# One transfer for the opening's weights, and x of stage 3's first 16 rows put together during stage 2

## The chip, the cores and the metric

The kernel runs on one core of a Trainium2 chip. The metric is the device time of one execution in microseconds (us). In what follows PE is TensorE, DVE VectorE, ACT ScalarE, POOL GpSimd and SP SyncE; SP, ACT and POOL also issue transfers (DMAs), each in the order of its own queue.

## What is computed

The input x has 384 x 384 positions of 128 channels in float32. Two layers follow one another:

```python
# layer 0
z = layernorm(x, norm_g, norm_b)
left  = (z @ Wl + bl) * sigmoid(z @ Wlg + blg)
right = (z @ Wr + br) * sigmoid(z @ Wrg + brg)
core = einsum('bikh,bjkh->bijh', left, right)
zo = layernorm(core, onorm_g, onorm_b) @ Wout + bout
x = x + sigmoid(x @ Wg + bg) * zo
# layer 1
left  = x @ W_left + b_left + x @ W_eq + b_eq
right_sum = sum(x @ W_right + b_right, axis=2)
out = (left * right_sum * sigmoid(x @ W_gate + b_gate)) @ W_out + b_out
y = layernorm(out + x, ln_scale, ln_bias)
```

## The kernel before, in words

The work is done in three stages, and nearly every instruction is pinned behind the one before it on its engine by `seq(...)`, so each engine and each DMA queue works in the order of the program.

**Stage 1** (0 to 1131 us) normalizes x and makes left and right for all 128 heads. It takes x in 288 steps of four rows by 128 positions. For each step DVE takes the statistics, POOL the reciprocal root (`powers`) and subtracts the mean (`shift`, or `first_step` for the first one), PE transposes four blocks and multiplies them by the weights `wz` (L331), ACT takes the sigmoid and DVE the product. The transposed, mean-free x goes to `xt_d` in HBM (`store_zt`), the subtracted values to `nd_d` (`store_nd`); x transposed is the sum of the two. Before the first step `fold` puts the layer norm's scale and shift into the weights. It needs the four weight matrices (`wst`), their biases (`brow`), and scale and shift as columns. Scale and shift come as two rows (`gb`), and PE turns them into columns (`pgb`, L165); DVE makes `g0`, their difference `d` and the matrix `m1` (L166 to L168); four small matmuls (L171, L172) follow, and `weights` (L179) writes `wz`. PE is kept going meanwhile with matmuls on a constant (`busy`, L156).

**Stage 2** (1131 to 1875 us) computes the core, one head h after the other: 18 matmul instructions (nine products, each recorded as two) at L501, 5.8 us a head. `load_h` (L93, L94, on SP) fetches left and right of a head three heads ahead into `lrh`; `fill` on POOL copies the right half into `rr` (L482, L483, and L476, L477 for a part that stayed on the chip); ACT copies the result to `ct` (L510) and squares it; DVE adds it to `csum` and `csq`; SP stores `ct` to `core_d` (L517). The last head is handled apart: its first 128 rows are copied, summed and stored first (L519 to L524), and the reciprocal root for them (`variance`, `root`, `inverse`, `newton`) is taken at once; POOL stores it (L533) and then sums the other rows of the last head (L534 to L536). The tiles "ve" and "r" of the pool `rp` have three buffers each.

**Stage 3** (1875 us to the end) goes through the 384 rows, row t in step t, with a software pipeline: `front` makes the gate of layer 0 for rows up to nine ahead, `scale_core(t)` multiplies the core by its reciprocal root, `layer0(t - 2)` finishes layer 0, `gated_left(t - 3)` and later `layer1` and `norm1` do layer 1. Rows are loaded in groups of RG = 4: `load_x` (SP) and `load_core` (SP). From row 16 (TR) on, x arrives transposed: `load_x` broadcasts `nd_d` into a tile (L576), and `add_x` has POOL issue an accumulating transfer of `xt_d` onto it (L584). The first 16 rows are loaded as they are (L570), PE transposes them in `front` (L640, three transposes a row), and ACT or DVE copies them out of PSUM (L642, L644). The core of rows 0 to 3 is loaded in two parts, since the last 16 heads are written last; for these rows PE spreads the root over the partitions (`pb`, L662) and DVE multiplies (L663), for later rows POOL does (L665). All loads at the start of stage 3 stand in one order on SP:

```python
for i0 in range(0, 3 * RG, RG):
    load_x(i0)
load_core(0)
load_x(3 * RG)
load_core(RG)
```

Of the kernel before, what the change touches and what calls it, by code (L numbers as in the profile page):

```python
# [14 lines left out]
P = 128  # L15
# [4 lines left out]
def triangle_then_gated_row_kernel(ctx: ExitStack, tc: tile.TileContext, a: dict, out: bass.AP):  # L20
# [10 lines left out]


    nc = tc.nc
    x = a["x"].rearrange("b i j c -> (b i) j c")
    y = out.rearrange("b i j c -> (b i) j c")
    N, _, C = x.shape
    H = a["L0_conv_Wl"].shape[1]
    assert C == P and H == P and N % P == 0
# [6 lines left out]
    A = 9  # L45
    L = 4
    TR = 16
# [6 lines left out]
    xt_d = dpool.tile([C, N, NB, P], F32, name="xt_d")  # L54
    nd_d = dpool.tile([N, N], F32, name="nd_d")

    def seq(ins):

        return tc.keep_in_program_order(ins)
# [4 lines left out]
    def load(dst, src, queue=nc.sync):  # L64
        seq(queue.dma_start(out=dst, in_=src))
# [15 lines left out]
    with ExitStack() as ctx2:  # L81
# [17 lines left out]
        with tc.tile_pool(name="p1w", bufs=6, side="right") as wp, \  # L99
# [25 lines left out]

            stage = lrp.tile([P, H, G, 2], F32, tag="lr", name="stage").rearrange("p h i s -> p (h i s)")
            wst, brow, gb = stage[:, 0:4 * H], stage[0:1, 4 * H:8 * H], stage[0:2, 8 * H:9 * H]
            m1, d = stage[:, 9 * H:10 * H], stage[:, 10 * H:10 * H + 1]
            sides = ("l", "r", "lg", "rg")
            for n, v in enumerate(("g", "b")):  # L130
                load(gb[n:n + 1], a["L0_conv_norm_" + v].rearrange("(o h) -> o h", o=1))
            for n, w in enumerate(sides):
                load(wst[:, n * H:(n + 1) * H], a["L0_conv_W" + w], nc.scalar)
            load_chunk(0, slice(4, XR))
# [7 lines left out]
            make_identity(nc, ident)  # L142
            for n, b in enumerate(sides):
                load(brow[:, n * H:(n + 1) * H], a["L0_conv_b" + b].rearrange("(o h) -> o h", o=1), nc.gpsimd)

# [3 lines left out]
            p0, p1 = (pps.tile([P, 2, 4 * H], F32, tag="pr", name=n)[:, 0] for n in ("p0", "p1"))  # L149
            pgb = tps.tile([P, 4, P], F32, tag="pt", name="pgb")[:, 0, 0:2]  # L150
            g0 = const([P, 1], "g0")

# [7 lines left out]
            def fold():  # L160

                busy(2)
                seq(nc.tensor.matmul(pgb, lhsT=gb, rhs=ident[0:2, 0:2], start=True, stop=True))  # L165
                seq(nc.vector.tensor_copy(g0, pgb[:, 0:1]))  # L166
                seq(nc.vector.tensor_sub(d, pgb[:, 1:2], g0))
                seq(nc.vector.tensor_scalar(m1, avg, d, None, ALU.mult))  # L168

                for p, gs in zip((p0, p1), halves):  # L170
                    seq(nc.tensor.matmul(p[:, gs], lhsT=m1, rhs=wst[:, gs], start=True, stop=False))  # L171
                    seq(nc.tensor.matmul(p[:, gs], lhsT=avg[0:1, :], rhs=brow[:, gs], start=False, stop=True))  # L172
# [278 lines left out]
        with tc.tile_pool(name="p2r", bufs=2, side="right", reuse_waits="tile") as rrp, \  # L451
# [14 lines left out]
            def fill(h):  # L466

                if h < H:
# [15 lines left out]
                    if h == 0:  # L484
                        stay()

            fill(0)
            for h in range(H):
                fill(h + 1)
                t, rr = loaded2.pop(h), right.pop(h)  # L490
                pc = ps.tile([P, NB, 512], F32, tag="pc", name="pc")
# [17 lines left out]
                if h < H - 1:  # L509
                    seq(nc.scalar.copy(ct, pc[:, :, :N]))  # L510
                    seq(nc.scalar.activation(sq, ct, AF.Square))
                    seq(nc.vector.tensor_add(csum, csum, ct))  # L512
                    seq(nc.vector.tensor_add(csq, csq, sq))
                    load_h(h + 3)

                    queue = nc.sync if h < H - 3 else nc.scalar
                    seq(queue.dma_start(out=to, in_=ct))  # L517
                else:
                    seq(nc.scalar.copy(ct[:, 0], banks[0]))  # L519
                    seq(nc.scalar.activation(sq[:, 0], ct[:, 0], AF.Square))  # L520
                    seq(nc.scalar.dma_start(out=to[:16, 0], in_=ct[:16, 0]))
                    seq(nc.scalar.dma_start(out=to[16:, 0], in_=ct[16:, 0]))
                    seq(nc.vector.tensor_add(csum[:, 0], csum[:, 0], ct[:, 0]))
                    seq(nc.vector.tensor_add(csq[:, 0], csq[:, 0], sq[:, 0]))  # L524
                    seq(nc.scalar.copy(ct[:, 1:], pc[:, 1:, :N]))
                    variance(0, slice(0, N))
                    root(0)
                    inverse(0, slice(0, N))
                    newton(0, slice(0, N))
                    seq(nc.scalar.dma_start(out=to[:, 1:], in_=ct[:, 1:]))  # L530


                    seq(nc.gpsimd.dma_start(out=rstd_d[0:P, :], in_=roots[0][1]))  # L533
                    seq(nc.gpsimd.tensor_tensor(sq[:, 1:], ct[:, 1:], ct[:, 1:], ALU.mult))  # L534
                    seq(nc.gpsimd.tensor_tensor(csum[:, 1:], csum[:, 1:], ct[:, 1:], ALU.add))
                    seq(nc.gpsimd.tensor_tensor(csq[:, 1:], csq[:, 1:], sq[:, 1:], ALU.add))  # L536
# [5 lines left out]
    with ExitStack() as ctx3:  # L542
# [3 lines left out]

        xp, lp, fp, inp = pool("p3x", 6), pool("p3l", 20), pool("p3f", A), pool("p3in", 3)
        wp, sp, op, up = pool("p3w", 4), pool("p3s", 4), pool("p3out", 3), pool("p3u", 18)
        ps2, ps = pool("p3ps2", 4, space=PSUM), pool("p3ps", 4, space=PSUM)
# [6 lines left out]

        def work_x(name):

            return lp.tile([P, N], F32, tag="x", name=name)

# [5 lines left out]
        def load_x(i0):  # L566

            if i0 < TR:
                xt = xin[i0] = xp.tile([P, RG, N], F32, tag="xt", name="xn")
                seq(nc.sync.dma_start(  # L570
                    out=xt.rearrange("p i (b c) -> p i b c", b=NB),
                    in_=x[i0:i0 + RG].rearrange("i (b p) c -> p i b c", p=P),
                ))
            elif i0 < N:
                xt = xts[i0] = xp.tile([P, RG, N], F32, tag="xt", name="xt")
                seq(nc.sync.dma_start(  # L576
                    out=xt.rearrange("p i j -> p (i j)"),
                    in_=nd_d[i0:i0 + RG].rearrange("i j -> (i j)").partition_broadcast(P),
                ))
# [8 lines left out]

        def load_core(i0):
            if i0 < N:  # L590
                ct = inp.tile([P, RG, N], F32, tag="ct", name="ct")

                for hs in (slice(0, H),) if i0 > 0 else (slice(0, H - 16), slice(H - 16, H)):
                    seq(nc.sync.dma_start(out=ct[hs], in_=core_d[i0:i0 + RG, hs].rearrange("i h j -> h i j")))
                rt = None
                if i0 > 0:
# [27 lines left out]
        def front(f):  # L624

            r = rows.get(f - L)
            if r:
                pg = bank("pg")
                seq(nc.tensor.matmul(pg[:, :N], lhsT=wg0, rhs=r["xT"], start=True, stop=True))  # L629
                gT = r["gT"] = work("gT", fp)  # L630
                seq(nc.scalar.activation(gT, pg[:, :N], AF.Sigmoid, bias=bg0))  # L631
            if f < N:
                i0, n = f // RG * RG, f % RG
                if f >= TR:
                    xT = xts[i0][:, n]
                else:
                    xT = work_x("xT")
                    pxt = ps2.tile([P, 512], F32, tag="py", name="pxt") if f < A else bank("pxt")
                    for s in cols:
                        seq(nc.tensor.transpose(pxt[:, s], xin[i0][:, n, s], ident))  # L640
                    if 4 <= f < A:
                        seq(nc.vector.tensor_copy(xT, pxt[:, :N]))  # L642
                    else:
                        seq(nc.scalar.copy(xT, pxt[:, :N]))  # L644
                rows[f] = {"xT": xT}

# [20 lines left out]
        def layer0(i):  # L667
# [7 lines left out]
            seq(nc.vector.scalar_tensor_tensor(pr[:, :N], pr[:, :N], bz, r["gT"], ALU.add, ALU.mult))  # L675
            x1T = r["x1T"] = work_x("x1T")
            seq(nc.vector.scalar_tensor_tensor(
# [108 lines left out]

        for i0 in range(0, 3 * RG, RG):
            load_x(i0)
        load_core(0)
        load_x(3 * RG)  # L790
        load_core(RG)

# [4 lines left out]
        for t in range(N + 3):  # L797

            while f < min(N + L, t + max(L, A - t // 3)):
                front(f)  # L800
                f += 1
            if t % RG == 0:
                load_core(t + 2 * RG)
            if t >= 2 and fetched <= f + 16:
                load_x(fetched)
                fetched += RG
# [63 lines left out]
    "x",  # L870
    "L0_conv_norm_g", "L0_conv_norm_b", "L0_conv_Wl", "L0_conv_bl", "L0_conv_Wlg", "L0_conv_blg",
    "L0_conv_Wr", "L0_conv_br", "L0_conv_Wrg", "L0_conv_brg", "L0_conv_onorm_g", "L0_conv_onorm_b",
    "L0_conv_Wout", "L0_conv_bout", "L0_conv_Wg", "L0_conv_bg",
# [22 lines left out]
```

## Time and profile before

| what | us |
|---|---|
| median of 3 runs (3287.99 to 3289.75) | 3288.08 |
| profiled execution, its own time | 3288.67 |
| span of the profiled execution (first to last instruction) | 3286.9 |
| PE busy in it | 3266.7 |
| first matmul of stage 1's products (L331) | 11.85 |
| first matmul of stage 2 (L501) | about 1131 |
| last matmul of stage 2 ends | about 1874.75 |
| first matmul of layer 0's output (L674) | 1886.24 |
| first gate matmul of layer 1 (L691) | 1888.51 |

The span is the time from the first to the last instruction; 1.8 us lie around it. Lines such as L331 are line numbers of the kernel before. A row of the profile names the engine, the line, what is written and what is read, how often, and how long; in brackets stands how long the engine was idle before it and which engine's instruction, or which transfer, ended that wait. Matmul records overlap, since they are pipelined: at full speed one product of 128 x 384 takes PE 0.645 us.

### The profile page before, as it was taken

Reading aid. Unit: us, or ns where it says so; the run is one execution under the profiler, and the core shown is the slowest. Engines: PE = TensorE matmul, PEld = TensorE weight load, DVE = VectorE, ACT = ScalarE, POOL = GpSimd, SP = SyncE. Lnnn points to the kernel's source line nnn. Section 1 sums busy time; section 2 is a strip of 40 time slices with the busy share of each in tenths; the row PEclk is TensorE's granted clock in tenths of the full one; section 3 lists DMA queues with packets and bytes.
Section 4 is the critical chain, followed back from the end, with each engine's and each line's share of the span. In section 5 each row is a group of like instructions: output and inputs, shape, how many; then the busy total and the mean of one; then the engine's idle time right before and its main releaser. Section 6 shows DMA issues by size and latency. Waiting matters only on the chain.

```text
span 3286.9 us, 48330 instructions
## 1 busy us (share of the span) xinstructions
PE 3266.7 (99%) x12460; PEld 1989.3 (61%) x12460; DVE 2489.0 (76%) x8022; ACT 1933.7 (59%) x4056; POOL 2280.3 (69%) x3301
## 2 busy tenths in 40 slices
PE   9999999999999999999999999999999999999998
PEld 4544444444444566666666666667777777777776
DVE  7777777777777655555555688888888888888888
ACT  4555555555555533333333467677777777777776
POOL 6555555555555555556666578888888888888997
PEclk9999999999999999999999999999999999999999
DMA  6998998999999499999999999999999999999994
GB/s 164 274 278 259 276 282 259 276 280 265 271 279 271 147 280 282 285 284 282 282 282 283 285 294 266 279 276 272 273 280 277 269 278 276 272 272 274 268 253 128
DMA packets 922055, 873.71 MB, mean 266 GB/s; under 512 B 24834, under 2 KB 836868, under 8 KB 921780
## 3 DMA queue, kind: packets, MB, share of 16 engines
q1 hardware_dynamic: 906532, 796.03, 78.5%
q0 software_dynamic: 13440, 72.56, 12.8%
q8 instruction: 102, 1.67, 0.2%
q10 hardware_dynamic: 1808, 2.03, 0.2%
q14 instruction: 173, 1.42, 0.1%
HBM read 508.63 MB, written 361.89 MB: 265 GB/s over the span
## 4 chain that ended last, share of the span: by engine, by line
PE 92%; POOL 5%; ACT 1%; issue 1%; DVE 1%; DMA 0%; POOLq 0%; ACTq 0%; DVEq 0%
PE pr L331 30%; PE pc L501 22%; PE py L703 7%; PE pg L629 6%; PE pl L692 6%; PE pr L674 6%; PE pg L691 6%; PE pt L279 4%; PE py L704 3%; POOL rs L723 1%; POOL yt L773 1%; POOL cs L665 1%; ACT py L738 1%; POOL nm L726 0%; POOL rs L722 0%
## 5 line engine op out<-in xcount | busy, mean ns | idle before, releaser
L331 PE MATMUL pr<-wz,zt 128*128 128x512 f32 x2304 | 1039.9, 593 | 0.0
L340 ACT ACTIVATE sg<-pr,rs 128x256 f32<-128x256 f32 x1152 | 482.9, 470 | 497.7 <-PE pr L331 363.8
L501 PE MATMUL pc<-rr,lrh 128*128 128x384 f32 x2304 | 743.3, 486 | 0.3 <-DVE lr L342 0.3
L342 DVE SCALAR_TENSOR_TENSOR lr<-pr,rs,sg 128x256 f32<-128x256 f32 x1152 | 504.6, 480 | 267.4 <-ACT sg L340 219.0
L331 PEld LDWEIGHTS pr<-wz,zt 128*128 128x128 f32 x2304 | 414.6, 191 | 410.7 <-issue 345.2
L501 PEld LDWEIGHTS pc<-rr,lrh 128*128 128x128 f32 x2304 | 452.4, 196 | 291.4 <-issue 1.1
L738 ACT ACTIVATE py<-py,nm,rs 128x128 f32<-128x128 f32 x1149 | 493.0, 430 | 197.8 <-POOL rs L727 116.8
L703 PEld LDWEIGHTS py<-wo,u 128*128 128x128 f32 x2304 | 376.8, 191 | 97.4
L512 DVE TENSOR_TENSOR csum<-csum,ct 128x1152 f32<-128x1152 f32 x127 | 179.1, 1410 | 337.9 <-ACT ct L510 337.9
L665 POOL TENSOR_TENSOR cs<-ct,rt 128x384 f32<-128x384 f32 x380 | 426.0, 1125 | 10.7 <-DMA rt<-rstd_d 5.4
L773 POOL TENSOR_TENSOR yt<-yt,lnb 128x384 f32<-128x384 f32 x380 | 423.8, 1117 | 3.1 <-DVE yt L767 3.1
L510 ACT COPY ct<-pc 128x1152 f32<-128x1152 f32 x127 | 142.1, 1119 | 445.3 <-PE pc L501 441.6
L703 PE MATMUL py<-wo,u 128*128 128x128 f32 x2304 | 402.1, 275 | 0.0
L260 POOL TENSOR_SCALAR sd<-mv 128x8 f32<-128x8 f32 (+1 forms) x145 | 28.5, 197 | 427.4 <-DVE mv L247 427.3
L270 POOL TENSOR_TENSOR z<-xt,nd 128x512 f32<-128x512 f32 x287 | 298.7, 1041 | 36.1 <-POOL z L270 30.9
L718 DVE BATCH_NORM_STATS2 st<-py 128x6 f32<-128x128 f32 x1152 | 265.6, 286 | 68.5 <-PE py L704 66.5
L704 PE MATMUL py<-ident,x1T 128*128 128x128 f32 x1152 | 314.1, 273 | 0.0
L674 PE MATMUL pr<-cs,wc 128*128 128x384 f32 x768 | 313.9, 491 | 0.0
L692 PE MATMUL pl<-x1T,mat_L_conv_W_left 128*128 128x384 f32 x768 | 311.0, 487 | 0.9 <-ACT gT L631 0.8
L691 PE MATMUL pg<-x1T,mat_L_conv_W_gate 128*128 128x384 f32 x768 | 310.8, 487 | 1.0 <-ACT g L694 0.9
L629 PE MATMUL pg<-xt,mat_L_conv_Wg 128*128 128x384 f32 x736 | 298.9, 488 | 1.3 <-ACT gT L631 1.3
L482 POOL COPY rr<-lrh 128x768 f32<-128x768 f32 x128 | 182.7, 1427 | 160.7 <-DMA lrh<-lr_d 160.2
(134 smaller groups left out, 4898.1 us busy)
## 6 DMA issues: line engine op xcount, KB each, us to landing
lr_d<-lr SPq DMA_DIRECT2D x128, 1024.0 KB, 7.2
lrh<-lr_d SPq DMA_DIRECT2D x128, 768.0 KB, 7.8
xt_d<-zt SPq DMA_DIRECT2D x288, 256.0 KB, 5.4
xt<-in_x_dram SPq DMA_DIRECT2D x143, 512.0 KB, 6.5
ct<-core_d SPq DMA_DIRECT2D x95, 768.0 KB, 6.2
rt<-rstd_d SPq DMA_DIRECT2D x95, 768.0 KB, 7.7
out_dram<-yt SPq DMA_DIRECT2D x94, 768.0 KB, 8.8
core_d<-ct SPq DMA_DIRECT2D x125, 576.0 KB, 8.8
```

The costliest lines, as they stand in the source:

```text
L331: seq(nc.tensor.matmul(pr[:, r, :], lhsT=zts[n, q][:, 2 * half + r, :], rhs=wz, start=True, stop=True))
L340: seq(nc.scalar.activation(sg[r], pr[:, r, 2 * H:], AF.Sigmoid, scale=rs[r]))
L342: seq(nc.vector.scalar_tensor_tensor(t[:, :, c * XR + r0 + r, :], pr[:, r, :2 * H].rearrange("k (h s) -> k h s", s=2), rs[r], sg[r].rearra ...
L501: seq(nc.tensor.matmul(banks[ib], lhsT=t[:, kb, ib * P:(ib + 1) * P, 0], rhs=rr[:, kb], start=(kb == 0), stop=(kb == NB - 1),))
L629: seq(nc.tensor.matmul(pg[:, :N], lhsT=wg0, rhs=r["xT"], start=True, stop=True))
L665: seq(nc.gpsimd.tensor_tensor(cs, ct[:, i % RG], rt[:, i % RG], ALU.mult))
L674: seq(nc.tensor.matmul(pr[:, :N], lhsT=wc, rhs=r["cs"], start=True, stop=True))
L691: seq(nc.tensor.matmul(pg2[:, :N], lhsT=wgate, rhs=r["x1T"], start=True, stop=True))
L692: seq(nc.tensor.matmul(pl[:, :N], lhsT=wleft, rhs=r["x1T"], start=True, stop=True))
L703: seq(nc.tensor.matmul(py[:, s], lhsT=r["u"][:, s], rhs=r["wo"], start=True, stop=False))
L738: seq(nc.scalar.activation(py[:, s], py[:, s], AF.Identity, bias=bias, scale=scale))
L773: seq(engine.tensor_tensor(yt, yt, lnbb, ALU.add))
```

## The change

It has two parts.

The first concerns the opening. The four weight matrices and the scale and the shift, as two more columns, are laid side by side on the host into `L0_side_W` (128 x 514), and the four biases into `L0_side_b`; each is loaded by one transfer on ACT's queue. Scale and shift arrive as columns, so the `pgb` matmul goes, and POOL instead of DVE makes `d` and `m1`.

The second concerns the first 16 rows of stage 3. In stage 2, `early_x(h)` puts x of row i together in three steps: at h = 5i + 6 SP broadcasts a row of `nd_d` into a "ve" tile, at h = 5i + 8 POOL issues an accumulating transfer of `xt_d` onto it, and at h = 5i + 11 SP stores it to a new tensor `xf_d` in HBM. Stage 3 loads these rows from `xf_d`, already transposed; the transposes and copies of `front` go, and the gate of row f is made in `front(f)` itself. The last head's first 128 rows are copied to a tile of their own, `last_h`, and stored whole; partition 127 of the first core tile (`ct`) comes straight from `last_h` by four transfers on POOL's queue, and the second part of the load fetches heads 111 to 126. The order of the first loads and the sizes of some pools change with it.

```diff
-            wst, brow, gb = stage[:, 0:4 * H], stage[0:1, 4 * H:8 * H], stage[0:2, 8 * H:9 * H]
...
-            for n, v in enumerate(("g", "b")):
-                load(gb[n:n + 1], a["L0_conv_norm_" + v].rearrange("(o h) -> o h", o=1))
-            for n, w in enumerate(sides):
-                load(wst[:, n * H:(n + 1) * H], a["L0_conv_W" + w], nc.scalar)
+            wst, g0, b0 = stage[:, 0:4 * H], stage[:, 4 * H:4 * H + 1], stage[:, 4 * H + 1:4 * H + 2]
+            brow, m1, d = stage[0:1, 5 * H:9 * H], stage[:, 9 * H:10 * H], stage[:, 10 * H:10 * H + 1]
+            load(stage[:, 0:4 * H + 2], a["L0_side_W"], nc.scalar)
+            load(brow, a["L0_side_b"].rearrange("(o h) -> o h", o=1), nc.scalar)
...
-            for n, b in enumerate(sides):
-                load(brow[:, n * H:(n + 1) * H], a["L0_conv_b" + b].rearrange("(o h) -> o h", o=1), nc.gpsimd)
...
-                seq(nc.tensor.matmul(pgb, lhsT=gb, rhs=ident[0:2, 0:2], start=True, stop=True))
-                seq(nc.vector.tensor_copy(g0, pgb[:, 0:1]))
-                seq(nc.vector.tensor_sub(d, pgb[:, 1:2], g0))
-                seq(nc.vector.tensor_scalar(m1, avg, d, None, ALU.mult))
+                seq(nc.gpsimd.tensor_tensor(d, b0, g0, ALU.subtract))
+                seq(nc.gpsimd.tensor_tensor(m1, avg, d.to_broadcast([P, P]), ALU.mult))
...
+            def early_x(h):
+                for n, step in enumerate((6, 8, 11)):
+                    i, odd = divmod(h - step, 5)
+                    if not odd and 0 <= i < TR:
+                        if n == 0:
+                            early[i] = rp.tile([P, N], F32, tag="ve", name="xe", bufs=NB)
+                            seq(nc.sync.dma_start(out=early[i], in_=nd_d[i].partition_broadcast(P)))
+                        elif n == 1:
+                            seq(nc.gpsimd.dma_start(
+                                out=early[i], in_=xt_d[:, i].rearrange("c b k -> c (b k)"), accum_op=ALU.add
+                            ))
+                        else:
+                            seq(nc.sync.dma_start(out=xf_d[:, i], in_=early.pop(i)))
...
+            last_h = rp.tile([P, N], F32, tag="r", name="last_h", bufs=NB)
             fill(0)
             for h in range(H):
                 fill(h + 1)
+                early_x(h)
...
-                    seq(nc.scalar.copy(ct[:, 0], banks[0]))
-                    seq(nc.scalar.activation(sq[:, 0], ct[:, 0], AF.Square))
-                    seq(nc.scalar.dma_start(out=to[:16, 0], in_=ct[:16, 0]))
-                    seq(nc.scalar.dma_start(out=to[16:, 0], in_=ct[16:, 0]))
-                    seq(nc.vector.tensor_add(csum[:, 0], csum[:, 0], ct[:, 0]))
+                    seq(nc.scalar.copy(last_h, banks[0]))
+                    seq(nc.scalar.activation(sq[:, 0], last_h, AF.Square))
+                    seq(nc.scalar.dma_start(out=to[:, 0], in_=last_h))
+                    seq(nc.vector.tensor_add(csum[:, 0], csum[:, 0], last_h))
...
-        xp, lp, fp, inp = pool("p3x", 6), pool("p3l", 20), pool("p3f", A), pool("p3in", 3)
-        wp, sp, op, up = pool("p3w", 4), pool("p3s", 4), pool("p3out", 3), pool("p3u", 18)
+        xp, lp, fp, inp = pool("p3x", 6), pool("p3l", 18), pool("p3f", A + 3), pool("p3in", 3)
+        wp, sp, op, up = pool("p3w", 4), pool("p3s", 4), pool("p3out", 3), pool("p3u", 17)
...
-        def load_core(i0):
+        def load_core(i0, between=None):
...
-                for hs in (slice(0, H),) if i0 > 0 else (slice(0, H - 16), slice(H - 16, H)):
+                for hs in (slice(0, H),) if i0 > 0 else (slice(0, H - 16), slice(H - 17, H - 1)):
                     seq(nc.sync.dma_start(out=ct[hs], in_=core_d[i0:i0 + RG, hs].rearrange("i h j -> h i j")))
+                    if i0 == 0 and hs.start == 0:
+                        for i in range(RG):
+                            seq(nc.gpsimd.dma_start(out=ct[H - 1:H, i], in_=last_h[i:i + 1]))
+                    if between and hs.start == 0:
+                        between()
...
         def front(f):
-            r = rows.get(f - L)
-            if r:
-                pg = bank("pg")
-                seq(nc.tensor.matmul(pg[:, :N], lhsT=wg0, rhs=r["xT"], start=True, stop=True))
-                gT = r["gT"] = work("gT", fp)
-                seq(nc.scalar.activation(gT, pg[:, :N], AF.Sigmoid, bias=bg0))
...
-                    for s in cols:
-                        seq(nc.tensor.transpose(pxt[:, s], xin[i0][:, n, s], ident))
...
+            r = rows[f] = {"xT": xts[f // RG * RG][:, f % RG]}
+            pg = ps2.tile([P, 512], F32, tag="py", name="pg") if f < A and f % 2 == 0 else bank("pg")
+            seq(nc.tensor.matmul(pg[:, :N], lhsT=wg0, rhs=r["xT"], start=True, stop=True))
+            gT = r["gT"] = work("gT", fp)
+            seq(nc.scalar.activation(gT, pg[:, :N], AF.Sigmoid, bias=bg0))
...
-        for i0 in range(0, 3 * RG, RG):
-            load_x(i0)
-        load_core(0)
+        load_x(0)
+        load_x(RG)
+        load_core(0, between=lambda: load_x(2 * RG))
+        load_core(RG)
         load_x(3 * RG)
-        load_core(RG)
...
-            while f < min(N + L, t + max(L, A - t // 3)):
+            while f < min(N, t + max(1, A - t // 2)):
...
-            if t >= 2 and fetched <= f + 16:
+            if t >= 2 and fetched <= t + 18:
```

More of the change, by code (lines that the diff above doesn't have):

```diff
@@ L36, in triangle_then_gated_row_kernel @@
     N, _, C = x.shape
-    H = a["L0_conv_Wl"].shape[1]
+    H = a["L0_side_b"].shape[0] // 4
     assert C == P and H == P and N % P == 0
@@ L45, in triangle_then_gated_row_kernel @@
     A = 9
-    L = 4
     TR = 16
@@ L55, in triangle_then_gated_row_kernel @@
     nd_d = dpool.tile([N, N], F32, name="nd_d")
+    xf_d = dpool.tile([C, TR, N], F32, name="xf_d")
     def seq(ins):
@@ L126, in triangle_then_gated_row_kernel @@
             stage = lrp.tile([P, H, G, 2], F32, tag="lr", name="stage").rearrange("p h i s -> p (h i s)")
-            wst, brow, gb = stage[:, 0:4 * H], stage[0:1, 4 * H:8 * H], stage[0:2, 8 * H:9 * H]
-            m1, d = stage[:, 9 * H:10 * H], stage[:, 10 * H:10 * H + 1]
-            sides = ("l", "r", "lg", "rg")
-            for n, v in enumerate(("g", "b")):
-                load(gb[n:n + 1], a["L0_conv_norm_" + v].rearrange("(o h) -> o h", o=1))
-            for n, w in enumerate(sides):
-                load(wst[:, n * H:(n + 1) * H], a["L0_conv_W" + w], nc.scalar)
+            wst, g0, b0 = stage[:, 0:4 * H], stage[:, 4 * H:4 * H + 1], stage[:, 4 * H + 1:4 * H + 2]
+            brow, m1, d = stage[0:1, 5 * H:9 * H], stage[:, 9 * H:10 * H], stage[:, 10 * H:10 * H + 1]
+            load(stage[:, 0:4 * H + 2], a["L0_side_W"], nc.scalar)
+            load(brow, a["L0_side_b"].rearrange("(o h) -> o h", o=1), nc.scalar)
             load_chunk(0, slice(4, XR))
@@ L149, in triangle_then_gated_row_kernel @@
             p0, p1 = (pps.tile([P, 2, 4 * H], F32, tag="pr", name=n)[:, 0] for n in ("p0", "p1"))
-            pgb = tps.tile([P, 4, P], F32, tag="pt", name="pgb")[:, 0, 0:2]
-            g0 = const([P, 1], "g0")
             def busy(n):
@@ L485, in fill @@
                         stay()
+            def early_x(h):
[11 more added lines that the diff above has]
+                            seq(nc.sync.dma_start(out=xf_d[:, i], in_=early.pop(i)))
+            early = {}
+            last_h = rp.tile([P, N], F32, tag="r", name="last_h", bufs=NB)
             fill(0)
@@ L555, in work @@
             return pool.tile([P, N], F32, tag=name, name=name)
-        def work_x(name):
-            return lp.tile([P, N], F32, tag="x", name=name)
         cols = [slice(b * P, (b + 1) * P) for b in range(NB)]
@@ L566, in load_x @@
         def load_x(i0):
[L568 to L574, printed above, removed]
+            if i0 < N:
                 xt = xts[i0] = xp.tile([P, RG, N], F32, tag="xt", name="xt")
@@ L577, in load_x @@
                     out=xt.rearrange("p i j -> p (i j)"),
-                    in_=nd_d[i0:i0 + RG].rearrange("i j -> (i j)").partition_broadcast(P),
+                    in_=xf_d[:, i0:i0 + RG].rearrange("c i j -> c (i j)") if i0 < TR
+                    else nd_d[i0:i0 + RG].rearrange("i j -> (i j)").partition_broadcast(P),
                 ))
@@ L624, in front @@
         def front(f):
-            r = rows.get(f - L)
-            if r:
-                pg = bank("pg")
-                seq(nc.tensor.matmul(pg[:, :N], lhsT=wg0, rhs=r["xT"], start=True, stop=True))
-                gT = r["gT"] = work("gT", fp)
-                seq(nc.scalar.activation(gT, pg[:, :N], AF.Sigmoid, bias=bg0))
[L632 to L638, printed above, removed]
-                    for s in cols:
-                        seq(nc.tensor.transpose(pxt[:, s], xin[i0][:, n, s], ident))
[L641 to L645, printed above, removed]
+            r = rows[f] = {"xT": xts[f // RG * RG][:, f % RG]}
[3 more added lines that the diff above has]
+            seq(nc.scalar.activation(gT, pg[:, :N], AF.Sigmoid, bias=bg0))
         def right_sums(i0, i1):
@@ L675, in layer0 @@
             seq(nc.vector.scalar_tensor_tensor(pr[:, :N], pr[:, :N], bz, r["gT"], ALU.add, ALU.mult))
-            x1T = r["x1T"] = work_x("x1T")
+            x1T = r["x1T"] = work("x1T", lp)
             seq(nc.vector.scalar_tensor_tensor(
@@ L870 @@
     "x",
-    "L0_conv_norm_g", "L0_conv_norm_b", "L0_conv_Wl", "L0_conv_bl", "L0_conv_Wlg", "L0_conv_blg",
-    "L0_conv_Wr", "L0_conv_br", "L0_conv_Wrg", "L0_conv_brg", "L0_conv_onorm_g", "L0_conv_onorm_b",
+    "L0_side_W", "L0_side_b", "L0_conv_onorm_g", "L0_conv_onorm_b",
     "L0_conv_Wout", "L0_conv_bout", "L0_conv_Wg", "L0_conv_bg",
@@ L885 @@
     nc = bacc.Bacc("TRN2", target_bir_lowering=False, num_devices=1)
+    sides = ("l", "r", "lg", "rg")
+    columns = [inputs["L0_conv_W" + s] for s in sides] + [inputs["L0_conv_norm_" + v][:, None] for v in "gb"]
+    inputs["L0_side_W"] = np.concatenate(columns, axis=1)
+    inputs["L0_side_b"] = np.concatenate([inputs["L0_conv_b" + s] for s in sides])
     arrays, aps = {}, {}
```

## The prediction

> **What bounds the kernel now.** I read the page's busy rows first, then the slices, the chain of waits at both seams, and the instructions around them.
>
> ```profile
> PE 3266.7 (99%) x12460; PEld 1989.3 (61%) x12460; DVE 2489.0 (76%) x8022; ACT 1933.7 (59%) x4056; POOL 2280.3 (69%) x3301
> ...
> DMA  6998998999999499999999999999999999999994
> ```
>
> PE is busy for 99% of the span, so time falls only where PE work is dropped or a PE gap closes. The DMA engines are at 9 tenths nearly everywhere. Chain of waits, opening (start, us, what):
>
> ```profile
> 1.04 3.78 PE p L156 x4
> 4.83 0.53 PE pgb L165 x2
> ...
> 5.76 0.30 DVE stage L168
> 6.06 0.04 issue
> 6.10 1.22 PE p L171 x2
> ...
> 11.85 1.22 PE pr L331
> ```
>
> PE warms on `avg`, then waits for scale and shift, and starts the real work at 11.85. At the seam of stages 2 and 3 the POOL queue reads (start, us; idle before it and releaser at the end):
>
> ```profile
> 1866.37 1.54 POOL L483 COPY rr<-lrh 128x256 f32<-128x256 f32 x1
> 1880.99 0.67 POOL L533 DMA_DIRECT2D rstd_d<-r  x1 [13.07 <-DVE r L449]
> 1881.68 1.48 POOL L534 TENSOR_TENSOR sq<-ct 128x768 f32<-128x768 f32 x1
> 1883.11 1.82 POOL L535 TENSOR_TENSOR csum<-csum,ct 128x768 f32<-128x768 f32 x1
> 1884.88 1.81 POOL L536 TENSOR_TENSOR csq<-csq,sq 128x768 f32<-128x768 f32 x1
> ```
>
> L534's input was ready at 1875.6 (L525's end), yet it ran at 1881.7: POOL keeps program order and stood behind L533. In stage 2 the stretch 1200 to 1800 (us, PE, PEld, DVE, ACT, POOL busy, clock, DMA share, GB/s) and its waits say:
>
> ```profile
> 1200.00:1800.00 600.00, 600.00 (x1862) 365.40 (x1861) 322.59 (x207) 235.81 (x207) 361.85 (x622) 1.00 0.92 283
> ```
> ```profile
> POOL rr L482 <- DMA lrh<-lr_d: 134.2, 96, 2.3
> POOL rr L477 <- PE pc L501: 102.2, 104, 2.1
> ```
>
> PE never waits there, but 8% of DMA time is all that is free, and POOL, which prepares the next head, waits for its load at nearly every head and then waits about 1.0 us for PE.
>
> **What the Trainium skill says.** "DMA: Bandwidth & Descriptors", section "Issuing engines are not separate DMA queues": transfers of all issuing engines run on the same 16 DMA engines and interleave. The trace agrees: in stage 3 the POOL queue's accumulates take 31.8% and the other queue 65.8% of them. Same page, "Anatomy of one DMA — SWDGE (gpsimd) path": about 2.0 us fixed for a POOL-issued transfer; here the small ones of the opening took 3.3 to 4.2. "TensorE: Matmul & The Clock Gate", "Part 1: The HAM clock gate": after an idle window of about 3.4 us PE falls to half clock. The trace agrees: the last matmul ends at 3273.2 and the granted clock goes from 1.00 to 0.50 at 3277.0.
>
> **Opening.** Removed: four weight transfers on ACT, two on SP, four on POOL, the pgb matmul (0.53 us) and three DVE steps. Added: one 257 KB transfer on ACT issued at 0.73, one of 2 KB behind it, and two POOL steps. When does the big one land? Wl (64 KB, same issue) landed 2.7 us after issue, Wlg 3.9 after its later issue, at 5.7; the 256 KB of x issued at 0.73 released DVE at 3.78. Two of these side by side: I take 4.2 (from 3.4 to 5.7). d costs 0.2 (L262's kind), m1 0.5 (L445, 128x128: 0.46), so L171 starts near 5.0 instead of 6.1: 1.1 us. Bounds: +1.3 gain (PE's own warm-up ends at 4.83), 0.5 loss. On POOL the steps of `powers` stand behind d and m1; they run at 5.17 now, and z was ready at 8.31 for transposes at 10.7, so 1 us there is hidden. Matmuls are at half speed until 14.3 (0.84 against 0.43 us at L331); if that instant stays where it is, the earlier start is worth half. I take **-0.9**.
>
> **Stage 2.** Added for each of 16 rows, over five heads: a broadcast (192 KB) and a store (192 KB) on SP, and an accumulate (192 KB) on POOL. POOL's issue is 0.91 us (L584), behind the fill and in the 1.0 us that it waits for PE: nothing. SP waits 4.2 us a head for PE: its two issues are hidden, and the store comes three heads after the accumulate (17.4 us; such transfers land in 9.4, at most 12.6), so SP isn't held. The price is DMA time. By the queue table the plain queue moved 796.03 MB in 78.5% of 3286.9 us, 308 GB/s; the POOL queue 72.56 MB in 12.8%, 172 GB/s. So 0.393/308 + 0.197/172 = 1.28 + 1.14 = 2.4 us per five heads, where 8% of 29.0 us, 2.2, are free. The queue becomes full but hardly more. A load may come about 1.4 us later than its median before PE sees it: POOL's 1.0 us of waiting (never under 0.78), and copies L482 and L483 that take 2.0 instead of 2.6 us when they come late, since DVE is then done. The peak delay by my sum is 1.3 minus the 0.4 that a head leaves free, plus a rest: 0.9 to 1.2. I take **+1.0** in all; nothing at best, rival 2 at worst.
>
> **The seam.** Removed from PE: 48 transposes, 16 rows of 0.324 us, 5.2 us; with them 16 copies on ACT and DVE, which are off the path. SP no longer waits 5.9 us at L594 for the last core's first rows; but the changed second transfer overlaps row 111 of the first, so it waits for that one (issued at 1871.0, 10.8 us), which makes it no earlier than now. load_x(12) moves behind rt of row 4 (1887.6); its row is wanted at t=7, near 1900, and I cost it at nothing. Row 127 of ct now comes by four POOL transfers, and these are issued after stage 2's last POOL work: at 1886.69, not when last_h is there (1873.2). At 0.5 us an issue and 3.3 to landing (the opening's), row 0 is whole at 1890.0; low 1888.7 (2.0 of the skill), high 1893.3 (6.6, as rstd_d). scale_core(0) (L663), at 1883.2 today, waits for it on DVE; behind it stand two more L663, L675 and L677, and PE's pr(0). Then 3 x 0.55 + 0.63 + 0.67: the first gate matmul of layer 1 (L691) runs at 1892.95 instead of 1888.51, 4.4 us later. Against that, PE has then done four more L629 (11 rows of gate against 7; 0.645 each, 2.6) and owes no transposes where before it still owed five rows (1.6): 4.2. Net **+0.2** (-1.1 to +3.5). PE's work before pr(0) (10 L629, 3 L662 from 1875.6) ends near 1885, so it idles 5 us, over the 4 us after which the clock fell at the end of the trace. Falling to half and returning costs 2 us or so (2.4 us of half rate were seen at L331 before the return, half of it lost, up to 4); even odds: **+1.0**.
>
> Buffers: gT gets 12 instead of 9, x1T 18 instead of a shared 20, u 17 instead of 18; a row's x1T and u are read 17 and 16 steps after they are written, so no new wait: nothing. Should one be short, layer 1 is late next.
>
> **Sum:** -0.9 + 1.0 + 0.2 + 1.0 = +1.3 on the profiled execution's 3288.67, 3290.0; the median of the runs is 0.6 lower, so I forecast 3289.4. A measurement of this kernel tells about 0.2%, 6.6 us, from no change. By itself this case spans 3286 to 3294.
>
> **Rivals.** (1) The direct transfers are there in time: POOL runs its three steps faster without DVE beside it, or they overtake. Then cs(0) is bound by the second ct transfer, at 1882.7 as now, and PE keeps its 4.2 us of lead plus 1.9 from an earlier pr(0) (1884.05 against 1886.24): -0.9 + 1.0 - 6.1, 3282. For it: last_h is ready 13 us before. Against: L534 shows that POOL doesn't overtake. (2) Stage 2 becomes bound by its loads: slower. Place: L482 waits for lrh, then L501 for rr. Each five heads the broadcast and store of one head push a load by 1.28 past a slack of 0.9, and the accumulate by the rest: 0.66 us, times 16, 10.6; without any recovery 16 x 2.4 = 38.7. It decides once the median landing of lrh (8.0 after issue) passes 9.4. For it: the free 8% are less than the 8.3% added. Against: stage 3 holds 97% share with PE busy. -0.9 + 10.6 + 1.2: 3299. (3) The opening does not do what it says: the transfer lands at 5.7, behind x, and the 0.9 is lost; 3290.3, inside the forecast.
>
> **Chances.** Forecast with (3) 0.62, rival 1 0.14, rival 2 0.24. The range 3282.3 to 3300 reaches to both. Faster by over 0.2% (below 3281.5) takes half of rival 1 and a little else: 0.09; slower (over 3294.7) nearly all of rival 2 and the forecast's tail: 0.27; within: 0.64.
>
> **What would show it.** Right: L171 near 5.0; no pxt; lrh landing near 9 and PE still gapless in 1200 to 1800; four POOL issues at 1886 to 1889; L663 waiting for DMA; a PE gap of some 5 us ahead of the first L674. Wrong: POOL issues before L533, a seam without the gap, or L501 waiting for L482 or L483.

## The result, and the profile after

The changed kernel takes 3297.65 us (median of 10 runs, 3296.2 to 3299.91) against 3288.05 us before (median of 10): a ratio of 1.0028, 95% interval 1.002 to 1.0037. It is 9.6 us slower. The profiled execution took 3298.65 with a span of 3296.9, 10.0 more than before. Its lines have moved: L670 is the former L674 (layer 0's output), L687 the former L691 (layer 1's gate), L659 the former L663 (`scale_core`, which writes `cs`), L639 the former L629 (layer 0's gate), L658 the former L662 (`pb`), L545 to L548 the former L533 to L536, L514 the former L501, L324 the former L331.

From the page after, the engines' busy time, the DMA slices, and the group of L670 (the last two columns: idle time of PE just before it, and what ended it):

```profile
PE 3265.0 (99%) x12410; PEld 1984.1 (60%) x12410; DVE 2484.6 (75%) x8014; ACT 1928.6 (58%) x4045; POOL 2288.5 (69%) x3319
...
DMA  6998998998998599999999889999999999999994
...
L670 PE MATMUL pr<-cs,wc 128*128 128x384 f32 x768 | 315.2, 492 | 9.6 <-DVE cs L659 9.6
```

PE's busy time fell by 1.7 us, yet the span grew by 10: there is one new wait of 9.6 us ahead of L670, and it is for DVE's `cs`. The transposes that went (5.2 us of PE by the prediction's count) do not show fully in the busy time, since other work ran at half clock, as the windows show below.

The opening, from the chain of waits after (start, us, what):

```profile
4.59 0.20 POOL stage L160
4.80 0.07 issue
4.87 0.41 POOL stage L161
5.28 0.04 issue
5.32 1.22 PE p L164 x2
...
11.07 2.07 PE pr L324 x2
```

The fold's first product runs at 5.32 instead of 6.10, and the first real product at 11.07 instead of 11.85. The first matmul of stage 2 comes at 1130.86 instead of 1131.46: 0.6 us gained, and the last one of stage 2 is still 0.6 us early. Stage 2 has cost nothing.

At the seam, POOL and DVE read (start, us; in brackets the idle time before and what ended it); the last line is DVE's first `cs` in the kernel before:

```profile
1880.40 0.59 POOL L545 DMA_DIRECT2D rstd_d<-r  x1 [12.94 <-DVE r L442]
...
1884.19 1.80 POOL L548 TENSOR_TENSOR csq<-csq,sq 128x768 f32<-128x768 f32 x1
1885.93 2.02 POOL L602 DMA_DIRECT2D ct<-last_h  x4
```
```profile
1891.93 0.55 DVE L659 TENSOR_TENSOR cs<-ct,pb 128x384 f32<-128x384 f32 x1 [11.84 <-DMA ct<-last_h]
```
```profile
1883.20 0.55 DVE L663 TENSOR_TENSOR cs<-ct,pb 128x384 f32<-128x384 f32 x1
```

The chain of waits shows how this reaches PE (start, us, what):

```profile
1884.24 1.69 POOL csq L548
1885.93 5.83 DMA ct<-last_h
...
1891.93 0.57 DVE cs L659
1892.50 0.14 issue
1892.64 1.62 PE pr L670 x2
```

`last_h` is written at 1872.1 to 1872.6, but the four transfers out of it are issued from 1885.93, behind the last sum, and the first row lands 5.8 us later, at 1891.8. (A landing time counts here from the start of the issue.) DVE has stood idle for 11.84 us by then, and PE, which ran out of work at 1883.1, stands until 1892.64. The windows of stage 2 (while the early rows are made) and of the seam (us; PE, PEld, DVE, ACT, POOL busy; granted clock; DMA share; GB/s), and then one of the kernel before:

```profile
1165.00:1625.00 460.00, 460.00 (x1427) 279.80 (x1427) 250.21 (x158) 180.78 (x159) 287.99 (x493) 1.00 0.98 302
1880.00:1895.00 15.00, 5.42 (x14) 2.61 (x12) 2.29 (x5) 1.98 (x4) 8.19 (x9) 0.74 0.84 268
1895.00:1910.00 15.00, 14.33 (x37) 7.96 (x37) 9.30 (x21) 4.23 (x8) 5.92 (x7) 0.80 0.80 283
```
```profile
1880.00:1895.00 15.00, 14.72 (x59) 8.92 (x57) 10.47 (x23) 7.02 (x15) 8.55 (x8) 1.00 0.86 286
```

In stage 2 PE is busy for all of 460 us with the DMA share at 0.98. At the seam the clock column falls below 1: the clock records of the trace have it at one half from 1887.3 to 1901.0, so PE's work from 1892.6 on is done at half rate for 8.4 us, and at most 4.2 of them are lost. The first gate matmul of layer 1 runs at 1898.93 instead of 1888.51, 10.4 us late; by row 100 it is 9.2 late; the end is 10.0 late.

### The profile page after: what moved, and what is told of

The parts are those of the page before. It is cut to its first block, busy times and chain, and to the rows that moved or that the text cites. A ratio compares the mean times of both kernels' runs of the same rounds, so it can differ in the third digit from the quotient of the medians.

```text
span 3296.9 us, 48292 instructions
## 1 busy us (share of the span) xinstructions
PE 3265.0 (99%) x12410; PEld 1984.1 (60%) x12410; DVE 2484.6 (75%) x8014; ACT 1928.6 (58%) x4045; POOL 2288.5 (69%) x3319
## 4 chain that ended last, share of the span: by engine, by line
PE 88%; POOL 7%; DVE 2%; ACT 1%; issue 1%; DMA 0%; POOLq 0%; DVEq 0%; ACTq 0%
PE pr L324 30%; PE pc L514 22%; PE py L699 6%; PE pr L670 6%; PE pl L688 6%; PE pg L687 6%; PE pg L639 6%; PE pt L272 4%; PE py L700 3%; POOL rs L719 2%; POOL yt L769 2%; POOL cs L661 2%; ACT py L734 1%; POOL xt L588 0%; DVE st L714 0%
## 5 line engine op out<-in xcount | busy, mean ns | idle before, releaser
L324 PE MATMUL pr<-wz,zt 128*128 128x512 f32 x2304 | 1040.0, 593 | 0.0
L514 PE MATMUL pc<-rr,lrh 128*128 128x384 f32 x2304 | 743.3, 486 | 0.3 <-DVE lr L335 0.3
L324 PEld LDWEIGHTS pr<-wz,zt 128*128 128x128 f32 x2304 | 414.2, 190 | 411.1 <-issue 345.9
L514 PEld LDWEIGHTS pc<-rr,lrh 128*128 128x128 f32 x2304 | 452.0, 196 | 291.8 <-issue 1.1
L670 PE MATMUL pr<-cs,wc 128*128 128x384 f32 x768 | 315.2, 492 | 9.6 <-DVE cs L659 9.6
L639 PE MATMUL pg<-xt,mat_L_conv_Wg 128*128 128x384 f32 x768 | 311.2, 488 | 2.1 <-ACT gT L641 1.8
L687 PE MATMUL pg<-x1T,mat_L_conv_W_gate 128*128 128x384 f32 x768 | 311.3, 487 | 0.9 <-ACT g L690 0.9
```

The costliest lines, as they stand in the source:

```text
L324: seq(nc.tensor.matmul(pr[:, r, :], lhsT=zts[n, q][:, 2 * half + r, :], rhs=wz, start=True, stop=True))
L514: seq(nc.tensor.matmul(banks[ib], lhsT=t[:, kb, ib * P:(ib + 1) * P, 0], rhs=rr[:, kb], start=(kb == 0), stop=(kb == NB - 1),))
L670: seq(nc.tensor.matmul(pr[:, :N], lhsT=wc, rhs=r["cs"], start=True, stop=True))
L687: seq(nc.tensor.matmul(pg2[:, :N], lhsT=wgate, rhs=r["x1T"], start=True, stop=True))
```

## The experiments

The theories were these. **A**: the four direct transfers are late because they stand behind POOL's sums in its queue; PE idles and loses its clock. **B**: such a transfer is slow in itself. **C**: the early x does the harm, because the transposes that it takes from PE had covered the wait.

Each ratio below is to the kernel before as it was measured beside that run (medians of 3289.62 us for the first four, 3288.74 for the last three); it is taken over all executions, and is not quite the quotient of the medians. Line numbers are those of the run's own kernel; `cs` is the scaled core, `pr` the product that makes layer 0's output, `pg` a gate.

### The direct transfers on ACT's queue

```diff
-    seq(nc.gpsimd.dma_start(out=ct[H - 1:H, i], in_=last_h[i:i + 1]))
+    seq(nc.scalar.dma_start(out=ct[H - 1:H, i], in_=last_h[i:i + 1]))
```

> The changed kernel (3297.7), with the four direct transfers of the last core issued on ACT's queue, where nothing stands ahead of them after 1875.6. Theory A (queue order: they are late because POOL issues them only at 1885.9, behind L545 to L548; PE then idles 9.6 us and its clock falls): row 0 is whole by 1880, cs(0) is bound by pb(0) and the second part of ct (1882), the PE gap ahead of the first L670 shrinks from 9.6 to 2 us or less, no half clock, and 10 to 13 us come back: 3285 to 3288, also below the kernel before. Theory B (a transfer from one partition to another is slow in itself, 6 us wherever it is issued): it lands at 1882, so nearly the same here; the landing of these four tells, 6 us against some 3. Theory C (the early x does the harm, since PE lacks the transposes that covered the wait): the gap stays near 9 us, 3297.

Measured: 3285.27 us, 0.9991 of the kernel before (0.9983 to 0.9999), as A said. The four transfers are issued from 1877.4; the first is there at 1880.4, and PE's wait for `cs` is gone and the clock stays full. All four landed after:

```profile
DMA to landing us min/median/max: 2.5/3.8/5.0
```

So issuing them earlier removes the loss. This edit changes the issuing engine too; the next run keeps it. A smaller wait came instead:

```profile
PE pg L639 <- DMA xt<-xf_d: 2.5, 1, 2.5
```

(The longest wait of PE in that kernel.) load_x(8) was held on SP for 10.4 us by the store of a stage 2 tile, and PE waited 2.5 us for its rows. `pb` stood behind this wait, so `cs` of row 0 started at 1885.88 and not at the 1882 that was expected. The profiled execution took 3288.5, more than ten of the 13 measured, and nine took 3284.1 to 3285.7; whether those had this wait is not known.

### POOL's three sums on DVE

```diff
-    seq(nc.gpsimd.tensor_tensor(sq[:, 1:], ct[:, 1:], ct[:, 1:], ALU.mult))
+    seq(nc.vector.tensor_tensor(sq[:, 1:], ct[:, 1:], ct[:, 1:], ALU.mult))
     ...
```

> The changed kernel, with POOL's three sums L546 to L548 done by DVE, which is idle then; the four direct transfers stay on POOL's queue, now right behind L545 at 1881.0. Theory A: issued from 1881.0, 4.9 us earlier, landing 3 to 4 us later since no big load has been issued yet: cs(0) at 1884.5 to 1885, PE gap 1.5 to 3 us, no half clock: 3286 to 3289. Theory B: landing takes 5.9 us again: cs(0) at 1887, gap near 5, perhaps half clock: 3289 to 3293. Theory C: no change, 3297.

Measured: 3288.82 us, 1.0001 (0.9992 to 1.0009), at the upper end of what A said. The transfers stay on POOL's queue, are issued 5.0 us earlier, from 1880.92, and `cs` of row 0 starts at 1885.18 instead of 1891.93, 6.75 us earlier. PE's gap is down to 2.8 us:

```profile
1885.79 0.91 PE L670 MATMUL pr<-cs,wc 128*128 128x384 f32 x2 [2.79 <-DVE cs L659]
```

(PE's instructions in order of time. The trace names nothing that released this `cs`; the first transfer landed at 1885.00.) Moving the issue by 5.0 moved the arrival by more: the first landing took 4.1 us instead of 5.8. With the engine and the queue unchanged, this run shows that the loss comes with the late issue. The half clock came all the same, from 1887.2 to 1890.6, which A had not expected of so short a gap:

```profile
1887.00:1891.00 4.00, 4.00 (x9) 2.22 (x8) 2.57 (x6) 0.58 (x1) 1.60 (x2) 0.57 0.96 319
```

### PE kept busy during the wait

```diff
+    if t == 2:
+        idle = ps2.tile([P, 512], F32, tag="py", name="idle")
+        for _ in range(13):
+            seq(nc.tensor.matmul(idle[:, :N], lhsT=wg0, rhs=xts[0][:, 0], start=True, stop=True))
     if 2 <= t < N + 2:
         layer0(t - 2)
```

> The changed kernel, with 13 matmuls of 128x384 put into PE's program ahead of the first L670, their output read by nothing (8.4 us at full clock, so they end before cs(0) is there). It takes away only the fall of the clock. If the fall to half clock costs what the records show (8.4 us of work at half rate, 4.2 lost): 3293.5. If the clock costs nothing beyond the wait: 3297.7. If the matmuls end after cs(0) they would cost what is over.

Measured: 3294.39 us, 1.0016 (1.0009 to 1.0024), near the 3293.5 expected if the fall of the clock costs what the records show. Its windows at the seam, to be held against those of the changed kernel, and the two lines that the reading rests on:

```profile
1880.00:1895.00 15.00, 13.13 (x41) 7.43 (x40) 2.32 (x5) 2.10 (x6) 8.14 (x9) 1.00 0.79 269
1895.00:1910.00 15.00, 14.97 (x47) 8.54 (x46) 12.16 (x27) 5.74 (x10) 7.22 (x8) 1.00 0.93 346
```
```profile
1892.73 1.48 DVE L659 TENSOR_TENSOR cs<-ct,pb 128x384 f32<-128x384 f32 x3 [12.52 <-DMA ct<-last_h]
```
```profile
1896.38 0.81 PE L687 MATMUL pg<-x1T,mat_L_conv_W_gate 128*128 128x384 f32 x2
```

The clock column stays at 1.00. `cs` of row 0 was even a little later (1892.73), but from there to the first gate matmul it took 3.65 us instead of 7.0: up to there the fall of the clock costs 3.35 us, apart from the wait. In the changed kernel the half clock goes on for 2.1 us after that matmul, which is about 1.0 more by the same count.

### The last core's rows through HBM, as before

```diff
-    for hs in (slice(0, H),) if i0 > 0 else (slice(0, H - 16), slice(H - 17, H - 1)):
+    for hs in (slice(0, H),) if i0 > 0 else (slice(0, H - 16), slice(H - 16, H)):
...
-            for i in range(RG):
-                seq(nc.gpsimd.dma_start(out=ct[H - 1:H, i], in_=last_h[i:i + 1]))
...
-    seq(nc.scalar.dma_start(out=to[:, 0], in_=last_h))
+    seq(nc.scalar.dma_start(out=to[:16, 0], in_=last_h[:16]))
+    seq(nc.scalar.dma_start(out=to[16:, 0], in_=last_h[16:]))
```

> The changed kernel without its direct transfers: the last core's first 16 rows are stored first and loaded back with heads 112 to 127, as in the kernel before; early x and the opening stay. Theory A: cs(0) near 1883 as in the kernel before, PE gap under 2 us, no half clock: 3284 to 3287, and 1 to 4 us below the kernel before. Theory C (missing cover): cs(0) near 1883 but the gap large all the same: 3291 or more.

Measured: 3283.4 us, 0.9983 (0.9977 to 0.999): the fastest kernel of the study, faster than both, and a little below the 3284 to 3287 that A said. `cs` of row 0 starts at 1882.38, set by PE's `pb` and not by a transfer:

```profile
1882.38 0.55 DVE L657 TENSOR_TENSOR cs<-ct,pb 128x384 f32<-128x384 f32 x1 [1.60 <-PE pb L656]
```

The two largest waits of PE in this kernel:

```profile
PE pg L637 <- ACT gT L639: 1.5, 2, 0.8
PE pg L637 <- ACT ct L538: 1.3, 1, 1.3
```

No wait for `cs` is left, so theory C falls in its plain form: without the transposes PE has enough to do, if the core is there in time. The change without its direct transfers is a gain of about 5.6 us (0.17%); the direct transfers turned it into a loss. The opening alone has no gain that can be measured (below), so nearly all of it belongs to the early x with the new order of loads and the new pools, which no run takes apart. The sum closes: this profile is 14.4 us shorter than that of the changed kernel, of which `cs` of row 0, 9.55 us sooner, and the clock, 3.35 and 1.0, make up 13.9.

### The direct transfers alone

The kernel before, with `last_h`, the four transfers on POOL's queue and heads 111 to 126 as the second part, and nothing else of the change.

> The kernel before with the direct transfers of the last core alone (last_h, four transfers on POOL's queue, heads 111 to 126 as the second part of ct); the transposes of the first 16 rows and the old opening stay. Theory A: POOL issues them at 1886.7, row 0 lands at 1891 to 1893 and the first layer 0 product, at 1886.24 in the kernel before, runs at 1892 to 1893.5; PE idles some 6 us, its clock falls, and with 2 to 4 us for that the kernel is 8 to 10 us slower than before: 3296 to 3299. Theory C (harm only where the transposes are gone): within 3 us of the kernel before.

Measured: 3298.3 us, 1.0026 (1.0016 to 1.0036), as A said. In the profiled execution stage 2 began 1.6 us later than before, and POOL issued the four transfers from 1888.26, later than expected; the first landed 4.9 us after that. PE's longest wait at the seam:

```profile
PE pr L677 <- DVE cs L666: 5.3, 1, 5.3
```

The loss is there with the transposes in place. They do matter in one way: with them PE waits 5.3 us and works at half clock for 3.8, without them it waits 9.6 and works at half clock for 8.4. So the two parts do not add up: 0.26% lost by the transfers alone and 0.17% gained by the rest would leave 0.09%, where 0.28% was measured. Early x gives PE less to do before the core arrives, and this turns into a longer gap.

### The opening alone

The kernel before with the new opening and nothing else.

> The kernel before with the new opening alone. The first fold product should run at 5.3 instead of 6.1, as in the changed kernel, and stage 2 should begin 0.3 to 1.5 us earlier, depending on when PE's clock rises: 3286.5 to 3289.5, not to be told from the kernel before by its time.

Measured: 3288.09 us, 0.9998 (0.999 to 1.0006). The first fold product runs at 5.27 and stage 2 begins at 1131.06, 0.4 us earlier. Where the clock rises differs from one execution to the next (13.3 to 17.1 us in the profiles of this study), which moves the start of stage 2 by more than the change does: with the old opening it was 1131.46 in one profile and 1133.09 in another. In this execution the clock was at full early, and PE waited 1.0 us for POOL's `z`, since POOL now makes `d` and `m1` first.

### More stores in stage 2

```diff
-    seq(nc.sync.dma_start(out=xf_d[:, i], in_=early.pop(i)))
+    seq(nc.sync.dma_start(out=xf_d[:, i], in_=early[i]))
+    for g in xg_d:
+        seq(nc.sync.dma_start(out=g[:, i], in_=early[i]))
...
```

> The changed kernel, with each of the 16 early rows stored to four more tensors that nothing reads: 0.79 MB more per five heads. By the prediction's prices that is 2.6 us of DMA time on top of 2.4, where 2.2 are free in 29.0: if these prices bound stage 2, PE waits 2.8 us per five heads, 45 us in all, and the time is 3330 to 3342. If the DMA engines have more room than their busy share tells, the changed kernel showing no wait at all in stage 2, it stays within 5 us of 3297.7.

Measured: 3297.72 us, 1.0025 (1.0015 to 1.0034), the same as the changed kernel within its spread, so the prices do not bound stage 2. Window of stage 2:

```profile
1165.00:1625.00 460.00, 460.00 (x1428) 279.81 (x1427) 242.66 (x158) 180.35 (x158) 273.17 (x493) 1.00 1.00 328
```

328 GB/s instead of 302, a share of 1.00, and PE still without a gap; loads of `lrh` land 7.8 us after issue in the median, as before (8.0). The profile (of an execution of 3295.35) also bears on theory B. Here SP's big loads happened to be issued at 1887.03, after the first direct transfer (1886.36); in the changed kernel they went out at 1885.63, ahead of it. DVE's `cs` of rows 0, 1 and 2:

```profile
1888.18 0.56 DVE L663 TENSOR_TENSOR cs<-ct,pb 128x384 f32<-128x384 f32 x1 [7.67 <-DMA ct<-last_h]
1891.18 0.56 DVE L663 TENSOR_TENSOR cs<-ct,pb 128x384 f32<-128x384 f32 x1 [2.44 <-DMA ct<-last_h]
1893.20 0.56 DVE L663 TENSOR_TENSOR cs<-ct,pb 128x384 f32<-128x384 f32 x1 [1.46 <-DMA ct<-last_h]
```

The four landed after:

```profile
DMA to landing us min/median/max: 1.6/4.9/5.8
```

The first transfer landed in 1.6 us, the slowest of the others, behind the loads, took 5.8, for the same 1.5 KB on the same queue. So such a transfer isn't slow in itself, and theory B falls. That the loads issued just before it slow it down is only argued, from their order in a few executions; no run held them back. Nor are they all of it: with POOL's sums on DVE the first one took 4.1 us, though SP had issued no load for 2.7 us before it, and the store of `rstd_d`, just ahead in the same queue, landed 0.2 us before it did.

## Why the prediction was right and where it was wrong

The time lies inside the range, but outside the likeliest case: 3289.4 was forecast, with 3286 to 3294 for that case, and 3297.65 measured; "slower by over 0.2%" had been given 0.27. It came out slower by the forecast's own mechanism, with terms too small, and not by rival 2, which was to carry the slow side and for whose sake the range reached to 3300. That the range holds the measured time is in this part luck.

**Opening: -0.9, measured -0.6.** The transfer released POOL at 4.6 (4.2 taken), L171's successor ran at 5.32 (5.0). PE is at half clock then, so of the early start of 0.8 only 0.4 counts, as the prediction itself said of a start at half speed; the other 0.2 is that the clock rose at 13.4 instead of 13.8, which differs between executions anyway. The 1 us on POOL that was called hidden is so only where the clock is low then: in the three profiles with a full clock early on, PE waits 0.7 to 1.0 us for `z`. Right in kind, and too small to be measured by time.

**Stage 2: +1.0, measured 0.** The working took the DMA engines' busy share for their load and found 8% free. At a share of 0.92 they moved 283 GB/s, at 1.00 they moved 328, with loads landing no later. So the busy share was no measure here of the room that was left. Rival 2 falls with this step, and its 0.24 of chance was misplaced.

**The seam: +0.2 net and +1.0 for the clock, measured about +10.** The order was foreseen: POOL's issues at 1885.9 (1886.7 said), `cs` waiting for them, a PE gap, a fall to half clock. The first gate matmul of layer 1 was forecast for 1892.95 and ran at 1898.93, 6.0 us later, and these are its parts:

- *Landing, 1.9.* `cs` was to start at 1890.0 and started at 1891.93. The 3.3 us came from the opening, where the DMA engines moved 176 GB/s meanwhile; here, at 282 GB/s, it took 5.8. SP's loads, released by `rstd_d` just before, were going out too; that they are the reason is likely and not shown.
- *From `cs` to the gate matmul, 0.7.* At full clock it takes 3.65 us (kept warm), where 2.95 was forecast.
- *Clock, 3.35.* It was given 1.0, the mean of "no fall" and 2 us. It fell, and cost 3.35 up to this matmul and about 1.0 after it, until 1901.0.

The lead of 4.2 us that was to be set against this was too large as well. Counted in the traces, from this matmul to that of row 20 PE does 13 gates of layer 0 instead of 16, and no transposes instead of those of five rows: 3.6 us, since one of the four gates stays ahead to the end. The kernel with the row through HBM gains 2.9 there (its shift goes from -1.9 to -4.8); the missing 0.7 was not located. The changed kernel gains the same if the 1.0 of half clock is added back (its delay goes from 10.4 to 8.5), and by row 100 it is at 9.2, since PE's waits in between are 0.7 us longer than before, most of it for ACT's `gT`.

The second part of the core, which the prediction let wait for row 111 of the first, waited for the store of head 126 instead; it landed at 1882.0 and bound nothing.

**The gap** was put at 5 us, from 1885 to 1890; it was 9.6, from 1883.1 to 1892.6. PE began its gates at once and so ran dry two us sooner, which earned nothing. The 4 us after which the clock was taken to fall, read from the end of the trace, are no threshold: with POOL's sums on DVE it fell after a gap of 2.8.

**Rival 1** (in time, 3282) did not happen here, but its price was close: with the transfers early on ACT's queue the time was 3285.27, with the row through HBM 3283.4. L534's lesson, that POOL does not overtake, held.

**Buffers and load_x(12)**, costed at nothing: no wait for them shows in the changed kernel. About 1 us of the end is later for another cause, behind DVE's last instruction; it is there in all kernels with early x (7.2 us from that instruction to the end with the row through HBM, 6.06 before) and stays open.

## What to carry to other kernels

A transfer is as early as its place in the issuing engine's queue: `last_h` was ready 13 us before its four small transfers could be issued, and with the longer way through HBM, on other queues, `cs` could start 9.55 us sooner. Take the landing time of a small transfer from a stretch like the one it will run in: here it was 1.6 to 6.5 us for the same bytes. And before work is taken off the bounding engine next to a seam, look at which arrival it was covering: if the arrival does not come earlier too, the saving becomes a gap, and on PE a gap may be paid a second time in clock.

## What the runs showed of the hardware that was not expected

- The clock fell to half after a gap of 2.8 us (POOL's sums on DVE), at 1887.2, when PE had already been at work again for 1.4 us; it came back 3.4 us later. After the gap of 9.6 us it stayed low for 13.7 us, from within the gap on. After gaps of 5.1 us (more stores) and 5.3 us (direct transfers alone) it stayed low for 10.2 and 6.8. All four times are multiples of 3.41 us, and the gap's length does not order them. Gaps of 1.3 (row through HBM), 1.9 (kept warm) and 2.5 us (ACT's queue) brought no fall.
- In three of the nine profiles (kept warm, row through HBM, opening alone) the clock was already full for 3.4 us from about 4 us on, fell to half for 6.8, and rose again at 14.4 to 14.9.
- DMA engines at a busy share of 0.92 could take 16% more bytes per second (283 to 328 GB/s) without a later landing of the loads that mattered (8.0 and 7.8 us in the median).
- The first of the four 1.5 KB transfers landed in 1.6 us while the DMA engines moved 14 GB/s (more stores), and in 3.0 to 6.5 us at 169 to 389 GB/s. The traffic alone does not order these: 4.9 us at 389 GB/s (direct transfers alone), 6.5 at 307 (kept warm).
